# Attention by head in one-bank tiles from one ring of seven, pair loads in 4096-byte pieces, new orders of all lists

## The chip, the cores and the metric

The kernel runs on 1 core of one Trainium2 chip. The metric is device time in microseconds (us) of one execution. Before the change three runs took 1517.64, 1525.69 and 1526.01 us, median 1525.69.

The engines are named as the profile names them: PE (matmul; its weight loads are PEld), DVE (vector), ACT (scalar, activations), POOL (GpSimd) and SP, which here only issues DMA transfers. SBUF is the working memory of 128 partitions; PSUM is the matmul accumulator, eight banks of 2048 bytes in each partition, so that a bank holds 512 floats.

## The reference

The input is `x` of 8 x 512 x 256 (batches, tokens, channels), all in float32. Four residual blocks follow each other, each on a layernorm of `x`:

```python
x = x + block_a(_layernorm(x))     # mamba mixer, then a feed-forward of 4 x 256
x = x + recurrent(_layernorm(x))   # gates over the batch index as time
x = x + attention(_layernorm(x))   # 16 heads of 16 channels, 512 tokens
x = x + recurrent(_layernorm(x))
```

The costly piece of the mamba mixer is a scan over tokens for every channel and each of 16 states:

```python
delta = softplus(dbc[..., :64] @ dt_proj_w + dt_proj_b)
h = exp(delta * A) * h + delta * xc * B       # for each of 16 states
y = einsum('ben,bn->be', h, C)
```

Attention makes, per head, `xw = x_h @ w_att_val`, scores `xw . x_h / sqrt(16)`, a softmax over 512 tokens and the product with `vx = x @ wv_w.T`.

## The kernel before

**Stage one (mamba of all batches, and the first recurrence).** 256 channels x 16 states make 4096 rows of one batch's scan; 128 partitions take 8 channels x 16 states, so a batch has 32 units. ACT makes `dl` (delta) and POOL (DVE for batch 0) makes `dx` (delta * xc), each 128 x 2 x 512. They are stored to DRAM by `store` in `mamba_in` (L338) and read back by `load_unit` (L384), which repeats 8 channels over 16 groups of partitions. A unit takes one load of `dl` and one of `dx`, each 128 pieces of 2048 bytes, 256 KB. Two units in a row share a tile (`dl_rep`, `dx_rep`: three tiles each). Then, per unit: ACT makes the decay `da = exp(A * dl)` into PSUM (`decay`, L391, three banks); POOL makes `bx = dx * B` for a pair of units (`increments`, L398, three tiles); DVE scans (`scan_unit`, L405) and multiplies by C (`times_c`, L411); PE sums the states of four units into `y` (`sum_states`, L421).

**Stage two (attention, with the second recurrence between it).** A step is one batch, one group of four heads and one block of 128 tokens. The scores are made twice: as queries against keys for the row maximum (`s` in the lists: PE L1104 into `ps_s`, `s_`: a DVE reduction into `mp`, L1386), and as keys against queries for the exponential (`e`: PE L1104 into `ps_e`, `e_`: ACT, L1403). A head has 16 channels, padded to 32 rows of PE, so a product uses a quarter of PE's rows. `scores` makes two heads at once into a tile of two banks; three such tiles (tag `two`) are six of the eight banks. All else (transposes, gates, projections) uses the seventh (tag `one`), and the values' sum `po` (`v`: PE L1124) the eighth. Maxima go back into the queries' padding (`m`: PE L1112, `m_`: DVE L1395), so the second product comes out with its maximum subtracted. `k0` to `k3` collect the outputs.

**Orders.** The order of every engine but POOL's own scheduling of waits is written out by hand: `FRONT` (batch 0 begins), `SLOTS` (seven times, one for each boundary), `LAST` and `REST` in stage one, `PROLOGUE`, `GAPS_01` (twice), `GAPS` (six times) and `END` in stage two. A word such as `dl`, `sc` or `e` makes the next piece of that kind; `i.` marks the input half of the next batch, `o.` the output half of the batch before, `e.` the layernorm of the batch after next, `q.` and `r.` the recurrence, `x.` transfers of `x`. Each engine, SP included, runs its own instructions strictly in that order; a wait holds all that stands behind it on the same engine. A tile of a pool is handed out in turn, and its next user waits until its last reader is done.

Of the kernel before, what the change touches and what calls it, by code (L numbers as in the profile page):

```python
# [15 lines left out]
P = 128  # L16
B = 8
# [7 lines left out]
QR = 4  # L25
HC = 8
# [151 lines left out]
def mamba_in(cx, a, t, b):  # L178
# [151 lines left out]
    def store(what, k):  # L330
        if not k:
            d = cx.dram.tile([KC, P, L], F32, tag=what, name=f"{what}_dram_{n}")
            setattr(t, what + "_d", d)
        to, x = (
            y[:, chunk(k), :]
            for y in (getattr(t, what + "_d").rearrange("k p l -> p k l"), getattr(t, what))
        )
        nc.sync.dma_start(to, x)  # L338
# [13 lines left out]
    for k in (None, 0, 1):  # L352
        on = "" if k is None else f".{k}"
        pieces["dx" + on] = lambda k=k: times_input(k)
        for what in ("dl", "dx"):
            pieces[f"store_{what}{on}"] = lambda what=what, k=k: store(what, k)
        if on:
            pieces["silu_x" + on] = lambda k=k: silu_xk(k)
# [9 lines left out]
def unit_channels(u):  # L368


    return u // 16, u % 4, u // 4 % 4


def load_unit(cx, t, b, u, what):

    k, j, r = unit_channels(u)
    pair = getattr(t, what + "_rep")
    if u % 2 == 0:
        pair[u // 2] = cx.rep.tile(
            [P, 2, L], F32, tag=what, bufs=3, name=f"{what}_rep_a{b}_{u}"  # L380
        )
    c0 = j * HP + r * CG
    src = getattr(t, what + "_d")[k, c0 : c0 + CG, :]
    cx.nc.sync.dma_start(  # L384
        pair[u // 2][:, u % 2, :], src.unsqueeze(0).to_broadcast([NS, CG, L])
    )
# [27 lines left out]
def sum_states(cx, a, t, b, quad):  # L414
# [5 lines left out]
    for j in range(4):  # L420
        cx.nc.tensor.matmul(  # L421
            t.y[k][head(j), :],
            a.sum[:, r, :],
            t.hc[4 * quad + j],
            start=False,
            stop=(r == QR - 1),
        )
# [195 lines left out]
def recurrent_step(cx, d, b, tok, tok_tag, ch, ch_tag, t=None, half=None):  # L623
# [9 lines left out]
    def bank(name, tag, bufs=None):  # L633

        if half is None:
            tag, bufs = cx.fill, None
        return cx.psum.tile([P, L], F32, tag=tag, name=name, bufs=bufs)
# [14 lines left out]
    def turn(k):  # L652
# [4 lines left out]
        ps = bank(f"ps_xT_{n}_{k}", ("one", "po")[k])  # L657
# [12 lines left out]
    def inputs(g, m):  # L670
        ps = bank(f"ps_{GATES[g][0]}{m}_{n}", "two", 3)
        ps_of[g, m] = gate_inputs(cx, ps, g, m, t.xT, tk, whole=(b == 0))
# [20 lines left out]
    def act_tile(g, m):  # L693
# [3 lines left out]
        return cx.att.tile([P, 2, L], F32, tag="e", bufs=4, name=f"{what}{m}_{n}")[:, 0, tk]  # L697
# [124 lines left out]
dx q.i0_ a.take_c y q.g0 sc o.gate1 cm i.rms x.load sc sc q.g0_ dl dl dl dx dl dl dl dx dx dx dx dx  # L822
dl dl dx dx dl dx dl dx dx dl da i.scale o.proj0 dx dx dl dx dl q.update0 dl dl o.proj1 i.turn0 q.f1
o.add_proj o.stats i.turn1 q.i1 da i.turn0_ q.f1_ sc i.turn1_ o.norm q.i1_ da cm cm cm q.hold1 y
o.turn0 bx bx e.stats bx bx bx o.residual c.bias bx bx bx o.turn1 o.turn0_ da sc sc o.turn1_ da
i.proj1 o.up0 o.up2 o.up1 da i.proj1_ o.up0_ da o.up2_ o.up1_ da da i.proj0 o.up3 o.up3_ i.proj0_ da
da e.center da sc cm sc cm i.conv1 cm sc da sc cm cm o.down1 y sc i.proj3 o.down0 x.half sc i.proj2
cm o.add1 i.conv0 sc cm sc cm i.silu_x i.silu_z y da i.xproj da i.xproj_ o.up4 dx dl dl dl dl dx dl
dx dx dx dx dl sc dl dx cm sc cm cm cm sc y i.dt1 sc o.add0 i.dt0 o.up5 o.up6 o.up7 da o.up4_ da
e.affine i.dt1_ i.dt0_ bx bx bx da i.dx da o.up5_ da o.up6_ da da o.up7_ da da e.outer da c.gate0 sc  # L830
cm sc cm cm cm sc sc cm y dx o.down3 o.down2 dl i.store_dl i.store_dx dx dl dl dx dl dx q.output0
i.rows dl q.g1 da e.square q.output0_ sc cm sc dx dx sc cm cm sc o.add3 cm cm o.add2 bx bx r.stats
bx e.residual sc sc q.g1_ r.norm cm cm q.update1 q.output1 y da r.turn0 y r.turn1 r.turn0_ da
r.turn1_ da r.f0 sc sc r.f0_ cm x.first sc r.i0 dl dl dx dl dx dl cm sc cm cm r.hold0 dx x.spill bx
da da q.output1_ bx dl dx da
# [4 lines left out]
da dl dx dx q.i0_ da da dl dx dx sc y o.gate1 o.proj0 o.proj1 q.g0 dx dl dl dl dx x.spill dl dx dl  # L840
q.f1 dl dx dl dx dl x.load dx dx q.i1 dl dx dx sc sc o.add_proj bx o.stats a.take_c sc q.g0_ o.norm
sc q.f1_ da cm q.update0 sc cm q.hold1 cm cm dx dl dl dx dl dl dl dx dx dx dl dx dx dl dx dl dl dl
dl dx dx dx dl o.turn1 dl dx dl dl dx o.turn0 y o.turn1_ o.turn0_ bx bx bx o.up0 da da bx o.residual
bx bx bx bx o.up3 o.up1 bx o.up4 o.up2 q.i1_ da o.up0_ da da da q.output1_ o.up3_ o.up1_ da da da
o.up2_ q.output0_ da da o.up4_ da r.output0_ cm sc cm sc sc cm sc cm cm cm sc y sc cm cm y o.down0
o.down1 o.up6 o.up5 o.up7 o.up6_ da da o.up5_ da o.up7_ da da sc sc cm cm sc sc sc o.add0 o.add1 sc
sc cm cm cm y q.output1 o.down2 r.output0 cm sc x.first sc cm cm o.add2 sc sc c.gate0 o.down3 o.add3
r.stats bx cm cm sc y q.g1 cm cm r.output1 r.norm r.turn0 da q.g1_ r.turn0_ q.update1 sc q.output0 y
bx bx bx r.turn1 r.turn1_ da da da r.f0 r.i0 da da da r.i0_ da r.f0_ r.g0 r.f1 r.i1 r.g0_ sc x.half
sc cm sc sc cm r.f1_ r.i1_ sc cm cm r.hold0 cm sc cm r.update0 sc y cm r.hold1 cm  # L850
# [3 lines left out]
o.bias y o.gate1 o.proj0 o.proj1 q.g1 o.add_proj.a o.stats.a o.add_proj.b o.norm.a o.turn0.a  # L854
o.turn1.a o.residual.b o.stats.b o.turn0_.a o.residual.a o.turn1_.a o.up2 o.up0 o.up1 q.g1_
q.output1_ o.up0_ o.up2_ o.up3 o.up1_ o.norm.b o.turn0.b o.up3_ o.turn0_.b o.down0 o.turn1.b o.down1
o.turn1_.b q.update1 o.up7 o.up4 o.add0 o.add1 o.up6 r.stats.a o.up5 o.up4_ o.up6_ o.up5_ r.norm.a
o.up7_ o.down2 o.down3 o.add2 o.add3 r.stats.b
# [3 lines left out]
i.stats i.outer i.center.a i.affine.a i.center.b i.affine.b i.square.a i.square.b i.residual i.rms  # L862
i.scale.a i.scale.b i.turn0 i.turn1 i.turn0_ i.turn1_ i.proj0 i.proj1 i.proj0_ i.proj1_ i.conv0
i.conv1 e.stats i.silu_x.0 i.silu_x.1 i.proj3 i.xproj i.xproj_ i.dt0 i.dt1 i.proj2 i.dt0_ i.dt1_
e.center i.dx.0 i.dx.1 i.rows e.affine i.store_dl.0 i.store_dx.0 i.store_dx.1 dl dx dx e.outer dl dl
da dx i.store_dl.1 e.square bx da da dx dl dx dx dl e.residual bx i.silu_z dx dl dx
# [3 lines left out]
def mamba_and_recurrence(cx, a, w, d):  # L870
# [31 lines left out]
    for b in (5, 6, 7):  # L902
# [3 lines left out]
        "dl": (UNITS, lambda b, n: load_unit(cx, T[b], b, n, "dl")),  # L906
        "dx": (UNITS, lambda b, n: load_unit(cx, T[b], b, n, "dx")),
# [91 lines left out]
def attention_in(cx, c, b, other=None):  # L999
# [6 lines left out]

    def bank(i):
        return other if other and i else cx.fill
# [28 lines left out]
    def turn(k, half):  # L1037
        on, tk, cs = part_of(half)
        ps = cx.psum.tile([P, L], F32, tag=bank(k), bufs=1, name=f"ps_xT_{n}_{k}{on}")
# [600 lines left out]
```

## Time and profile before

The profiled execution took 1520.85 us, of which 1519.1 us is the span from the first instruction to the last; the mean granted TensorE clock was 0.979.

| engine | busy us | share of the span | instructions |
|---|---|---|---|
| PE | 1437.2 | 95% | 6812 |
| PEld | 702.1 | 46% | 6812 |
| DVE | 1086.7 | 72% | 1628 |
| ACT | 836.0 | 55% | 1283 |
| POOL | 501.0 | 33% | 300 |

The costliest groups, as instruction, shape, count, total and mean of one:

| line, engine | what | count | busy us | mean ns |
|---|---|---|---|---|
| L1386 DVE | row maximum, 128x1024 | 256 | 305.5 | 1222 |
| L405 DVE | scan, 128x512 | 256 | 304.6 | 1214 |
| L398 POOL | `bx`, 128x1024 | 128 | 301.5 | 2368 |
| L1403 ACT | exponential of scores, 128x1024 | 256 | 255.2 | 1022 |
| L391 ACT | decay, 128x512 | 256 | 173.7 | 688 |
| L411 DVE | times C, 128x512 | 256 | 164.6 | 674 |
| L1104 PE | scores for `e` | 1024 | 226.3 | 630 |
| L1104 PE | scores for `s` | 1024 | 223.1 | 649 |
| L1124 PE | values | 1024 | 135.5 | 607 |
| L1395 DVE | maximum into queries, 128x512 | 32 | 21.9 | 685 |
| L1142 ACT | copy of `po`, 128x512 | 32 | 18.7 | 584 |

The DMA engines moved 196.77 MB in 112141 packets; the queue that SP issues on was busy for 46.7% of the span. A float32 product is two matmul instructions in the trace, so 512 products of a kind count as 1024. Busy time is the union of a group's instructions: four products that run side by side count once.

### The profile page before, as it was taken

To read this page: it belongs to the slowest core of one execution; us is meant where nothing else is said; L and a number is where in the kernel's file an instruction comes from. 1 tells how busy PE (TensorE), PEld (TensorE's weight loads), DVE (VectorE), ACT (ScalarE), POOL (GpSimd) and SP (SyncE) were. 2 spreads that over 40 slices of the span, in tenths; PEclk is the share of its full clock that TensorE was granted. 3 is DMA by queue.
4 is the path that set the end of the run, shared out by engine and by line. 5 is a ranking of instruction groups with operands and counts; after the bars stand their busy time and mean duration, and the time that the engine had idled before them with its cause. 6 is when DMAs were issued, how large, how long until landed. Compare 5 with 4: busy or idle time off the path is not lost.

```text
span 1519.1 us, 19714 instructions
## 1 busy us (share of the span) xinstructions
PE 1437.2 (95%) x6812; PEld 702.1 (46%) x6812; DVE 1086.7 (72%) x1628; ACT 836.0 (55%) x1283; POOL 501.0 (33%) x300
## 2 busy tenths in 40 slices
PE   4479999999999999999899999999999999999998
PEld 1125455655555555667334443334333333333347
DVE  4799999999999899833766767565656646555326
ACT  5666778676867665522255464645455444554522
POOL 2777777776768566512300000000000000000000
PEclk9699999999999999999799999999999999999999
DMA  7999999899999999703101100100110001110214
GB/s 233 265 260 247 266 241 281 235 265 258 258 260 254 238 253 266 203 1 114 56 19 45 41 17 23 37 19 15 37 23 26 22 15 34 23 37 8 79 68 139
DMA packets 112141, 196.77 MB, mean 130 GB/s; under 512 B 17201, under 2 KB 27761, under 8 KB 112041
## 3 DMA queue, kind: packets, MB, share of 16 engines
q1 hardware_dynamic: 109752, 188.52, 46.7%
q10 hardware_dynamic: 1824, 5.15, 1.0%
q0 software_dynamic: 464, 1.84, 0.3%
q8 instruction: 54, 0.88, 0.2%
q14 instruction: 47, 0.38, 0.1%
HBM read 163.24 MB, written 23.56 MB: 123 GB/s over the span
## 4 chain that ended last, share of the span: by engine, by line
PE 82%; DVE 10%; ACT 3%; issue 2%; DMA 2%; POOL 1%; SPq 0%; ACTq 0%; DVEq 0%; POOLq 0%
PE ps_e_c L1104 10%; PE ps_s_c L1104 10%; PE ps_o_c L1124 8%; PE ps_f_o L522 6%; PE ps_f_o L498 6%; DVE hc_a L405 3%; PE y_a L421 3%; PE ps_in_a L245 3%; PE ps_w_c L1204 2%; PE ps_f_d L599 2%; PE ps_i_d L599 2%; PE ps_g_d L599 2%; DVE hc_a L411 2%; PE ps_v_c L1070 2%; PE ps_f_d L612 2%
## 5 line engine op out<-in xcount | busy, mean ns | idle before, releaser
L1386 DVE TENSOR_REDUCE mp<-ps_s_c 128x2 f32<-128x1024 f32 x256 | 305.5, 1222 | 174.0 <-PE ps_s_c L1104 125.5
L1403 ACT ACTIVATE e_c<-ps_e_c 128x1024 f32<-128x1024 f32 x256 | 255.2, 1022 | 221.3 <-PE ps_e_c L1104 146.4
L398 POOL TENSOR_TENSOR bx_a<-dx_rep_a,B_a 128x1024 f32<-128x1024 f32 x128 | 301.5, 2368 | 107.0 <-DMA dx_rep_a<-dx_dram_a 55.7
L405 DVE TENSOR_TENSOR_SCAN hc_a<-da_a,bx_a 128x512 f32<-128x512 f32 x256 | 304.6, 1214 | 20.2 <-POOL bx_a L398 9.6
L391 ACT ACTIVATE da_a<-dl_rep_a,neg_a 128x512 f32<-128x512 f32 x256 | 173.7, 688 | 113.9 <-DMA dl_rep_a<-dl_dram_a 64.3
L1104 PE MATMUL ps_e_c<-q_c,keys 32*128 32x512 f32 x1024 | 226.3, 630 | 0.7 <-DVE q_c L1395 0.7
L1104 PE MATMUL ps_s_c<-keys,q_c 32*128 32x512 f32 x1024 | 223.1, 649 | 3.0 <-DVE mp L1386 1.7
L411 DVE TENSOR_TENSOR hc_a<-hc_a,Cp_a 128x512 f32<-128x512 f32 x256 | 164.6, 674 | 0.0
L85 POOL TENSOR_TENSOR rs_d<-ve_d,neg_half 128x4 f32<-128x4 f32 x8 | 8.1, 1015 | 404.1 <-DVE ve_d L84 212.9
L1124 PE MATMUL ps_o_c<-e_c,va 128*32 128x512 f32 x1024 | 135.5, 607 | 0.0
L498 PE MATMUL ps_f_o<-h_o,w 128*128 128x256 f32 x512 | 116.6, 381 | 1.3 <-ACT f_o L511 0.8
L1104 PEld LDWEIGHTS ps_e_c<-q_c,keys 32*128 32x128 f32 x1024 | 68.5, 183 | 101.4 <-issue 52.9
L522 PE MATMUL ps_f_o<-w,f_o 128*128 128x256 f32 x512 | 115.1, 381 | 0.0
L498 PEld LDWEIGHTS ps_f_o<-h_o,w 128*128 128x128 f32 x512 | 96.2, 190 | 28.6 <-ACT da_a L391 6.8
L522 PEld LDWEIGHTS ps_f_o<-w,f_o 128*128 128x128 f32 x512 | 96.4, 190 | 22.1 <-ACT da_a L391 5.0
L421 PE MATMUL y_a<-hc_a,sum 128*32 128x512 f32 x512 | 90.1, 625 | 15.5 <-DVE hc_a L411 15.5
L1104 PEld LDWEIGHTS ps_s_c<-keys,q_c 32*128 32x128 f32 x1024 | 65.8, 187 | 72.5 <-issue 29.9
L85 POOL TENSOR_TENSOR rs_c<-ve_c,neg_half 128x4 f32<-128x4 f32 x7 | 7.1, 1010 | 217.6 <-DVE ve_c L84 217.6
L511 ACT ACTIVATE f_o<-ps_f_o,vecs 128x256 f32<-128x256 f32 x128 | 53.0, 467 | 23.4 <-PE ps_f_o L498 23.4
L245 PE MATMUL ps_in_a<-hT_a,w_in 128*128 128x512 f32 x128 | 65.0, 638 | 0.4 <-ACT dl_a L307 0.4
L1124 PEld LDWEIGHTS ps_o_c<-e_c,va 128*32 128x32 f32 x1024 | 21.6, 108 | 89.6 <-issue 87.1
L115 PE MATMUL ps_hT_a<-ident,h_a 128*128 128x128 f32 x64 | 13.4, 332 | 37.0 <-ACT h_a L225 35.9
(317 smaller groups left out, 1974.8 us busy)
## 6 DMA issues: line engine op xcount, KB each, us to landing
dl_rep_a<-dl_dram_a SPq DMA_DIRECT2D x256, 256.0 KB
dx_rep_a<-dx_dram_a SPq DMA_DIRECT2D x256, 256.0 KB
x<-in_x_dram SPq DMA_DIRECT2D x8, 512.0 KB
keys<-xT_c SPq DMA_DIRECT2D x128, 32.0 KB
o_c<-oT_c SPq DMA_DIRECT2D x128, 32.0 KB
xT_dram_d<-xT_d SPq DMA_DIRECT2D x8, 512.0 KB
xT_back<-xT_dram_d SPq DMA_DIRECT2D x8, 512.0 KB
sum_c<-inverse_c SPq DMA_DIRECT2D x15, 256.0 KB
```

The costliest lines, as they stand in the source:

```text
L245: nc.tensor.matmul(ps, a.in_proj[:, k, ts(m, P)], t.hT[:, k, :], start=(k == 0), stop=(k == KC - 1))
L391: cx.nc.scalar.activation(t.da[u], t.dl_rep[u // 2][:, u % 2, :], AF.Exp, scale=a.A[:, u : u + 1])
L398: cx.nc.gpsimd.tensor_mul(t.bx[pair], t.dx_rep[pair], t.B.unsqueeze(1).to_broadcast([P, 2, L]))
L405: cx.nc.vector.tensor_tensor_scan(t.hc[u], t.da[u], t.bx[u // 2][:, u % 2, :], 0.0, ALU.mult, ALU.add)
L411: cx.nc.vector.tensor_mul(t.hc[u], t.hc[u], t.Cp)
L421: cx.nc.tensor.matmul(t.y[k][head(j), :], a.sum[:, r, :], t.hc[4 * quad + j], start=False, stop=(r == QR - 1),)
L498: nc.tensor.matmul(ps[:, m, :], a.w1[:, k, ts(m0 + m, P)], t.h2[:, k, ts(half, L // 2)], start=(k == 0), stop=(k == KC - 1),)
L522: nc.tensor.matmul(ps, t.f[c // 2][:, m, ts(c % 2, P)], a.w2[:, m, :], start=(m == 0), stop=(m == FC - 1),)
L1104: cx.nc.tensor.matmul(ps[:, j, :], lhs[rows, :], rhs[rows, :], start=True, stop=True)
L1124: cx.nc.tensor.matmul(po[head(j), :], c.va[b % 2][:, t, g * HG + j, :], es[j // 2][:, j % 2, :], start=(t == 0), stop=(t == TC - 1),)
L1386: nc.vector.tensor_reduce(c.mp[:, t, h : h + 2, DH], ps.pop(("s", b, g, t, i)), AX.X, ALU.max, negate=True)
L1403: nc.scalar.activation(e, ps.pop(("e", b, g, t, i)), AF.Exp)
```

## The change

1. **Pair loads.** The DRAM copies of `dl` and `dx` are laid out so that channels c and c + 64 of a chunk of 128 stand beside each other. One load then brings both units of a pair, in 128 pieces of 4096 bytes (512 KB), and there are 256 loads in place of 512. The units of a quad come in the order of `QUAD`; `A_log` and the rows of `y` follow it. The stores write 2 x 64 x 512 in DRAM from 128 partitions, always one chunk at a time: 32 stores of 256 KB in place of 4 of 256 KB and 14 of 512 KB.
2. **Attention by head.** `scores` makes one head into one bank. Each reduction, exponential and query copy is 128x512, and there are twice as many. All PSUM tiles of the stage but `po` come from one ring of seven banks (tag `bank`). The `e` tiles are eight of 128x512 in place of four of 128x1024.
3. **Orders.** All seven lists are new. In `SLOTS` the stores, written as `i.store_dl i.store_dx`, become four single ones.

No arithmetic is added or left out; POOL and PE run as many instructions as before (3630 products on PE), DVE 256 more, ACT 271 more, SP 242 fewer.

```diff
     def store(what, k):
         if not k:
-            d = cx.dram.tile([KC, P, L], F32, tag=what, name=f"{what}_dram_{n}")
+            d = cx.dram.tile([KC, P // 2, 2, L], F32, tag=what, name=f"{what}_dram_{n}")
             setattr(t, what + "_d", d)
-        to, x = (
-            y[:, chunk(k), :]
-            for y in (getattr(t, what + "_d").rearrange("k p l -> p k l"), getattr(t, what))
-        )
-        nc.sync.dma_start(to, x)
+        to = getattr(t, what + "_d")[k].rearrange("c h l -> h c l")
+        nc.sync.dma_start(to, getattr(t, what)[:, k, :])
...
-def load_unit(cx, t, b, u, what):
-
-    k, j, r = unit_channels(u)
-    pair = getattr(t, what + "_rep")
-    if u % 2 == 0:
-        pair[u // 2] = cx.rep.tile(
-            [P, 2, L], F32, tag=what, bufs=3, name=f"{what}_rep_a{b}_{u}"
-        )
+def load_pair(cx, t, b, pair, what):
+
+    k, r, j = pair // 8, pair // 2 % QR, pair % 2
+    rep = cx.rep.tile([P, 2, L], F32, tag=what, bufs=3, name=f"{what}_rep_a{b}_{2 * pair}")
+    getattr(t, what + "_rep")[pair] = rep
     c0 = j * HP + r * CG
-    src = getattr(t, what + "_d")[k, c0 : c0 + CG, :]
-    cx.nc.sync.dma_start(
-        pair[u // 2][:, u % 2, :], src.unsqueeze(0).to_broadcast([NS, CG, L])
-    )
+    src = getattr(t, what + "_d")[k, c0 : c0 + CG]
+    cx.nc.sync.dma_start(rep, src.unsqueeze(0).to_broadcast([NS, CG, 2, L]))
...
             t.y[k][head(QUAD[j]), :],
...
 SLOTS = """
...
-cm sc cm cm cm sc sc cm y dx o.down3 o.down2 dl i.store_dl i.store_dx dx dl dl dx dl dx q.output0
-i.rows dl q.g1 da e.square q.output0_ sc cm sc dx dx sc cm cm sc o.add3 cm cm o.add2 bx bx r.stats
...
+q.output0 dl dx sc q.g1 cm sc sc cm sc cm sc sc i.dx da sc cm o.add2 da q.output0_ bx c.bias o.add3
+q.output1 q.g1_ i.store_dx.0 i.store_dl.0 r.stats bx cm cm cm cm dl i.store_dl.1 i.rows dx
+i.store_dx.1 dx dl dx y y q.update1 r.norm r.turn0 r.turn1 r.turn0_ r.turn1_ r.f0 da da r.f0_ sc sc
+sc cm cm sc cm dx dl x.spill da q.output1_ da bx bx x.first r.i0 r.hold0 cm
...
-def scores(cx, name, lhs, rhs, i):
-
-    ps = cx.psum.tile([P, 2, L], F32, tag="two", bufs=3, name=f"{name}_{i}")
-    for j in range(2):
-        rows = head(2 * i + j)
-        cx.nc.tensor.matmul(ps[:, j, :], lhs[rows, :], rhs[rows, :], start=True, stop=True)
+def scores(cx, name, lhs, rhs, j):
+
+    ps = cx.psum.tile([P, L], F32, tag=cx.fill, name=f"{name}_{j}")
+    cx.nc.tensor.matmul(ps, lhs[head(j), :], rhs[head(j), :], start=True, stop=True)
     return ps
...
     def row_max_(b, g, t, i):
-        h = g * HG + 2 * i
-        nc.vector.tensor_reduce(
-            c.mp[:, t, h : h + 2, DH], ps.pop(("s", b, g, t, i)), AX.X, ALU.max, negate=True
-        )
+        to = c.mp[:, t, g * HG + i, DH : DH + 1]
+        nc.vector.tensor_reduce(to, ps.pop(("s", b, g, t, i)), AX.X, ALU.max, negate=True)
...
     def attend_(b, g, t, i):
-        e = cx.att.tile([P, 2, L], F32, tag="e", bufs=4, name=f"e_c{b}_{g}_{t}_{i}")
+        e = cx.att.tile([P, L], F32, tag="e", bufs=8, name=f"e_c{b}_{g}_{t}_{i}")
         nc.scalar.activation(e, ps.pop(("e", b, g, t, i)), AF.Exp)
...
-            cx.psum = pool(st2, "c_psum", 1, space=PSUM)
-            cx.fill = "one"
+            cx.psum = pool(st2, "c_psum", 7, space=PSUM)
+            cx.fill = "bank"
```

## The prediction

> **What bounds the kernel now.** I first cut the span where its character changes: the busy time of every engine in six stretches.
>
> ```profile
> core 0: us, PE busy (x) PEld busy (x) DVE busy (x) ACT busy (x) POOL busy (x), PEclk, DMA share, GB/s
> 0.00:52.00 52.00, 16.10 (x32) 6.34 (x32) 20.94 (x55) 31.47 (x58) 19.49 (x24) 0.87 0.77 243
> 100.00:576.00 476.00, 461.35 (x1859) 268.89 (x1860) 455.66 (x707) 338.16 (x602) 344.84 (x181) 0.99 0.99 256
> 760.00:1435.00 675.00, 672.23 (x3850) 256.24 (x3848) 402.41 (x536) 344.52 (x414) 28.65 (x26) 1.00 0.10 27
> ```
>
> From 100 to 576 us (mamba) DVE is busy for 455.66 of 476 us, and DMA's share is 0.99 at 256 GB/s. Two resources look full, so I asked what DVE waited for there:
>
> ```profile
> DVE hc_a L405 <- ACT da_a L391: 7.0, 11, 1.6
> DVE u_a L457 <- PE ps_op_o L445: 3.0, 4, 0.7
> DVE ps_g_b L712 <- ACT ps_g_b L618: 2.1, 4, 0.6
> ```
>
> The largest entry is 7.0 us, and none names a transfer. DVE is the bound; DMA is full but prefetched far enough ahead. The loads can give DVE at most the 7.0 us.
>
> From 760 to 1435 us (attention) PE is busy for 672 of 675 us. A busy PE need not be at its peak, so I looked at its order:
>
> ```profile
> 1005.87 0.70 PE L1104 MATMUL ps_e_c<-q_c,keys 32*128 32x512 f32 x2
> 1005.88 0.70 PE L1104 MATMUL ps_s_c<-keys,q_c 32*128 32x512 f32 x2
> 1006.40 0.59 PE L1104 MATMUL ps_e_c<-q_c,keys 32*128 32x512 f32 x2
> 1006.42 1.44 PE L1104 MATMUL ps_s_c<-keys,q_c 32*128 32x512 f32 x6
> 1007.79 1.06 PE L1124 MATMUL ps_o_c<-e_c,va 128*32 128x512 f32 x8
> 1008.78 1.14 PE L1104 MATMUL ps_s_c<-keys,q_c 32*128 32x512 f32 x8
> 1009.75 1.02 PE L1104 MATMUL ps_e_c<-q_c,keys 32*128 32x512 f32 x4
> 1010.70 0.64 PE L1124 MATMUL ps_o_c<-e_c,va 128*32 128x512 f32 x4
> ```
>
> Each score product is two matmul instructions on one group of 32 rows. Four products on four groups run side by side: from 1008.78 the x8 take 0.97 us before the next x4 start, and those two products alone take 0.95. So a run of scores costs rounds, not products. Six products in two rounds last 1.92 us (1008.78 to 1010.70); the eight instructions of values before them last 0.99. With 0.86 us a round, 0.2 remains for each change between the 32-row form and another. Attention is this sum, with hardly any wait.
>
> **The attention part.** I counted PE's order in both programs from the first score to the last values. Before: 210 runs of scores holding 296 rounds, 139 runs of full-array products, 115 of values. After: 182 runs, 289 rounds, 68 full-array runs, 123 of values. Rounds: 7 x 0.86 = 6.0 us. Runs of scores: 28 x 0.2 = 5.6. Full-array runs: 71 x 0.18, if they change as dearly as the scores do, = 12.8. Values: 8 x 0.13 = 1.0 back (0.99 less one round). Together -23.4 us.
>
> The price is in the evacuations, which double in number. The 128x1024 reduction takes 1222 ns; a 128x512 read of PSUM on DVE takes about 685 (the addition at L1395), so 256 x (2 x 685 - 1222) = +38 us on DVE. On ACT the exponential goes from 1022 to about 584 (the 128x512 copy at L1142): 256 x 146 = +37 us. Against 675 us DVE goes to 440 and ACT to 382, both beside PE, whose order hides them while banks come free in time. A ring of seven hands out banks strictly in turn, so the late evacuation of any one holds PE. After counts 71 runs of seven scores, which use the whole ring. A wait of 0.07 us for each is +5; I take -18 us, with ends -23 and 0.
>
> **The loads.** 512 loads of 128 pieces of 2048 bytes become 256 loads of 128 pieces of 4096. In the mamba stretch the SP queue moved 117.98 MB in 96.2% of 16 x 476 us, that is 127 ns for 2048 bytes. For 4096 I use a lone transfer at 1461 us (window 1.8 us), and for the number of engines a lone one at 844 us (window 2.3 us from 843.90, its first line the busy tenths in forty slices). The lines of the SP queue in the three DMA views:
>
> ```profile
> q1 hardware_dynamic: 64856, 117.98, 96.2%
> ```
> ```profile
> DMA packets 144, 0.52 MB, mean 291 GB/s; under 512 B 16, under 2 KB 16, under 8 KB 144
> ...
> q1 hardware_dynamic: 144, 0.52, 71.2%
> ```
> ```profile
> DMA  0000099020212244464375446446423320320000
> ...
> DMA packets 136, 0.26 MB, mean 114 GB/s; under 512 B 8, under 2 KB 8, under 8 KB 136
> ...
> q1 hardware_dynamic: 136, 0.26, 35.8%
> ```
>
> The first lone one (128 pieces of 4096): 0.712 x 16 x 1.8 / 128 = 160 ns each. So the loads fall from 512 x 128 x 0.127 / 16 = 520 us of the engines to 256 x 128 x 0.160 / 16 = 328. DVE did not wait for them, so that buys part of the 7.0 us: -3 (0 to -7).
>
> The Trainium skill, DMA: Bandwidth & Descriptors, Specifications, puts the least size for line rate at 512 bytes; by that rule pieces of 4096 would gain nothing over 2048. Here a byte in 4096 cost 39 ps against 62 in the loaded stretch, so the measurement decides; by the page's rule the term of -3 would be 0.
>
> **The stores** are where I expect the loss. To let two channels stand side by side in DRAM, each store now writes 2 x 64 x 512 from 128 partitions: its outermost count is 2, where it was 128. The second lone transfer is `sum_c<-inverse_c` (L1188), whose source is 8 x 16 x 512. It has 8 small completion packets; the first, 128 rows on both sides, has 16. So 8 outermost ran on 8 engines, and I read 2 as two engines. A store of 128 pieces of 2048 bytes is then 64 pieces on each of two, not 8 on each of sixteen. A piece costs between 80 ns (half of 160) and 103 (0.358 x 16 x 2.3 us / 128, in the lone transfer at 844 us); I take 90, nearer the lone rows, since fourteen engines are idle then: 5.8 us a store.
>
> The Trainium skill, same page, section "Why a DMA increments its semaphore by 16 and not by 1", says that a transfer takes the largest number up to 16 that divides the outermost counts of both sides. For 2 and 128 this is 2; it speaks against this change.
>
> Four such stores stand at each batch boundary, and everything behind them on those two rings waits. After's order on SP: store dx.0, store dl.0, load dl of pair 0, store dl.1, B, C, load dx of pair 0, store dx.1, load dx of pair 1. From the first issue (0 us; 1.4 us to the first packet: L1188 was issued at 842.80, and its first busy slice begins at 844.19): two stores end at 13.0. SP sits in the wait of the dl load meanwhile, with all that follows queued behind it. That load: 1.4 to start, 8 x 0.16 to move, 15.8. Store dl.1: 21.6. B and C, 16 x 0.09: 23.0. dx of pair 0: 24.3. POOL's product (2.37): 26.7, and only then can the new batch's first scan start. Then dx.1 to 30.1, dx of pair 1 to 31.4, its product to 33.8.
>
> What covers this is DVE's own work. At the first issue POOL has just made dx, two products of 2.37 after the scan of unit 21; in DVE's order there remain 7 scans at 1.13 (start to start), 10 products with C at 0.59, two residual additions (0.7), statistics (2.3), three gate products (1.8) and the copy of C (0.6): 19.2 us. Before, the same stretch was covered: store at 479.67, first new scan at 499.05, no wait. Now DVE stands from 19.2 to 26.7 = 7.5 us, then from 29.6 (two scans and a gate) to 33.8 = 4.2. 11.7 us at 7 boundaries = +82. With 80 ns a piece the same sum gives 8.8 x 7 = +62; with 103, 15.1 x 7 = +106.
>
> In the front, two stores (13.0 us) precede the first dx load: first scan 18.2 us after the first store against 11.8 before (35.09 to 46.88), and the third store delays pair 1 by about 3 more: +9 (0 to +16).
>
> The other reordering (rms, conv, LAST, REST) moves the same instructions; from 576 to 760 us DVE's main wait is 25.9 us for `ps_f_o`, which stays PE's. I cost it at 0 and include +-5.
>
> **Sum:** 82 + 9 - 18 - 3 = +70 on the profiled 1520.85 us (span 1519.1 and 1.75 around it; 0.3% under the median of 1525.69): 1591 us.
>
> **Rivals.** (1) The stores are not slow: they spread over four engines or more. With four (2.9 us a store) the first scan could start at 18 us, inside the 19.2, so this is the point from which it decides. Left are -18, -3 and 0 to -5: 1497 us, faster. For it: no transfer here shows an outermost 2. Against: 8 gave 8.
> (2) The ring holds PE: with the stores hidden, 0.3 us at each of the 71 runs of seven = +21, which cancels the -23: 1516 us, no change. Against: DVE and ACT have a third of the stretch free.
> (3) DVE's cover is longer than 19.2 because it runs late at the boundary: the stall shrinks to the second one, 4.2 x 7 = 29, with +9 - 21: 1538.
>
> **Numbers.** Stores slow and exposed: 75%, own range 1555 (62 + 4 - 25 - 7) to 1643 (106 + 16). Rival 1: 17%, rival 2: 6%, rival 3: 2%. The range for 8 in 10 must reach into rival 1: 1497 to 1643. About 1% (15 us) is what a measurement of this kernel tells from no change: faster 0.17, same 0.07, slower 0.76.
>
> **What would show it.** After's stores with 2 small completion packets, 5 to 7 us long on an eighth of the engines; DVE's waits at `hc_a` for POOL's `bx_a` or ACT's `da_a` near 80 us from 50 to 600 us, twice a boundary; attention 15 to 23 us shorter. I am wrong if the stores land in under 3 us, if DVE stays at 96% between the boundaries and at them, or if PE shows waits at the scores for DVE or ACT of over 20 us.

## The result, and the profile after

The changed kernel takes 1699.48 us (median of 4, 1697.93 to 1702.38) against 1525.47 for the kernel before beside it: a ratio of 1.1156, 95% interval 1.1117 to 1.1196. The forecast was 1591 with a range up to 1643: the direction held, the size did not. The profiled execution has a span of 1696.1 us.

| us | before | after | difference | predicted |
|---|---|---|---|---|
| up to the first scan | 46.9 | 53.5 | +6.6 | +9 |
| first scan to the first score | 682.7 | 882.5 | +199.8 | +79 (stores 82, loads -3) |
| first score to the last values | 702.9 | 673.7 | -29.2 | -18 |
| the rest | 86.6 | 86.4 | -0.2 | 0 |

The same cut of the span as before the change; mamba now runs to about 780 us, and attention from 960. Columns: busy time and instructions of each engine, granted clock, DMA share, GB/s.

```profile
core 0: us, PE busy (x) PEld busy (x) DVE busy (x) ACT busy (x) POOL busy (x), PEclk, DMA share, GB/s
0.00:52.00 52.00, 14.62 (x32) 5.86 (x32) 18.05 (x52) 28.58 (x55) 15.27 (x22) 0.87 0.64 204
100.00:780.00 680.00, 527.98 (x1910) 297.19 (x1910) 476.67 (x728) 346.50 (x616) 355.63 (x185) 0.87 0.77 188
960.00:1600.00 640.00, 638.87 (x3796) 264.92 (x3794) 425.34 (x787) 355.93 (x663) 32.17 (x28) 1.00 0.10 27
```

DVE, which bounded mamba, is now idle for 203 of 680 us there (680 - 476.67), where it was idle for 20 of 476. DMA's share has fallen too, from 0.99 to 0.77: the transfers are neither the full resource they were nor ahead of the work. In attention PE is as busy as it was, in a shorter stretch. What DVE waits for from 100 to 780 us (us in total, times, longest):

```profile
DVE hc_a L393 <- ACT da_a L379: 61.4, 21, 12.4
DVE hc_a L393 <- POOL bx_a L386: 45.1, 13, 8.9
DVE Cp_a L320 <- DMA C_a<-bc_a: 29.5, 5, 13.8
DVE act_f_b L689 <- ACT ps_f_b L606: 24.9, 9, 5.6
```

The scan (`hc_a`) waits for ACT's decay and POOL's product, and these wait for loads. Their lines before, then after (count, busy us, mean ns; then the engine's idle time before them, and what ended most of it):

```profile
L391 ACT ACTIVATE da_a<-dl_rep_a,neg_a 128x512 f32<-128x512 f32 x256 | 173.7, 688 | 113.9 <-DMA dl_rep_a<-dl_dram_a 64.3
L398 POOL TENSOR_TENSOR bx_a<-dx_rep_a,B_a 128x1024 f32<-128x1024 f32 x128 | 301.5, 2368 | 107.0 <-DMA dx_rep_a<-dx_dram_a 55.7
```
```profile
L379 ACT ACTIVATE da_a<-dl_rep_a,neg_a 128x512 f32<-128x512 f32 x256 | 169.8, 686 | 318.2 <-DMA dl_rep_a<-dl_dram_a 273.1
L386 POOL TENSOR_TENSOR bx_a<-dx_rep_a,B_a 128x1024 f32<-128x1024 f32 x128 | 300.5, 2355 | 314.5 <-DMA dx_rep_a<-dx_dram_a 272.3
```

The copy of C waits for its load, which stands behind the stores on SP. PE's granted clock fell as well, from 0.99 to 0.87, but DVE waits for PE itself for only 13.5 of the 203 us. One boundary on SP's queue (start, duration of the issue, what is issued), and the DMA engines' work while SP is silent:

```profile
324.13 0.54 SPq L336 DMA_DIRECT2D dx_dram_a<-dx_a  x1
324.73 0.53 SPq L336 DMA_DIRECT2D dl_dram_a<-dl_a  x1
338.75 0.58 SPq L374 DMA_DIRECT2D dl_rep_a<-dl_dram_a  x1
339.38 0.51 SPq L336 DMA_DIRECT2D dl_dram_a<-dl_a  x1
339.93 0.57 SPq L314 DMA_DIRECT2D B_a<-bc_a  x1
```
```profile
DMA  1111111111111111111111111111111111111111
...
DMA packets 202, 0.41 MB, mean 51 GB/s; under 512 B 2, under 2 KB 2, under 8 KB 202
...
q1 hardware_dynamic: 202, 0.41, 13.1%
```

Between 324.73 and 338.75 SP issues nothing: the load of `dl` waits for the store that it reads. The second view is 329 to 337 us within that gap: 51 GB/s at a share of 13.1%, that is 2.1 of 16 engines. SP's waits of that kind from 60 to 800 us (us in total, times, longest):

```profile
SPq L374 <- DMA dl_dram_a<-dl_a: 95.9, 8, 14.8
```

The stores do run on two engines, as the Trainium skill has it (DMA: Bandwidth & Descriptors, "Why a DMA increments its semaphore by 16 and not by 1") and as the prediction took it: 200 pieces in 8 us on two engines are 80 ns each, 5.1 us for a store of 128 (predicted 5.8).

### The profile page after: what moved, and what is told of

The parts are those of the page before. It is cut to its first block, busy times and chain, and to the rows that moved or that the text cites. A ratio compares the mean times of both kernels' runs of the same rounds, so it can differ in the third digit from the quotient of the medians.

```text
span 1696.1 us, 19885 instructions
## 1 busy us (share of the span) xinstructions
PE 1458.0 (86%) x6812; PEld 739.3 (44%) x6812; DVE 1107.3 (65%) x1884; ACT 852.8 (50%) x1554; POOL 498.8 (29%) x300
## 4 chain that ended last, share of the span: by engine, by line
PE 55%; DMA 25%; POOL 6%; DVE 5%; ACT 5%; SPq 2%; issue 2%; ACTq 0%; POOLq 0%; DVEq 0%
DMA dx_rep_a<-dx_dram_a 10%; PE ps_e_c L1085 9%; DMA dl_rep_a<-dl_dram_a 9%; PE ps_s_c L1085 8%; PE ps_o_c L1105 7%; DMA dl_dram_a<-dl_a 6%; POOL bx_a L386 4%; PE ps_f_o L486 3%; PE ps_v_c L1053 2%; PE ps_w_c L1185 2%; PE ps_f_o L510 2%; DVE hc_a L393 2%; PE ps_f_d L587 2%; PE ps_g_d L587 2%; PE ps_i_d L587 2%
## 5 line engine op out<-in xcount | busy, mean ns | idle before, releaser
L1374 DVE TENSOR_REDUCE mp<-ps_s_c 128x1 f32<-128x512 f32 x512 | 324.9, 683 | 162.8 <-PE ps_s_c L1085 140.5
L1389 ACT ACTIVATE e_c<-ps_e_c 128x512 f32<-128x512 f32 x512 | 279.7, 600 | 168.2 <-PE ps_s_c L1085 105.9
L1085 PE MATMUL ps_e_c<-q_c,keys 32*128 32x512 f32 x1024 | 289.0, 626 | 0.0
L1085 PE MATMUL ps_s_c<-keys,q_c 32*128 32x512 f32 x1024 | 279.7, 626 | 0.6 <-DMA keys<-xT_c 0.6
L409 PE MATMUL y_a<-hc_a,sum 128*32 128x512 f32 x512 | 104.7, 673 | 46.5 <-DVE hc_a L399 46.5
L1085 PEld LDWEIGHTS ps_e_c<-q_c,keys 32*128 32x128 f32 x1024 | 98.5, 183 | 84.4 <-issue 34.0
L1085 PEld LDWEIGHTS ps_s_c<-keys,q_c 32*128 32x128 f32 x1024 | 95.1, 183 | 78.8 <-issue 22.8
L433 PE MATMUL ps_op_o<-w_op,zs_a 128*128 128x256 f32 x128 | 49.7, 548 | 91.6 <-ACT act_i_b L606 51.5
L433 PEld LDWEIGHTS ps_op_o<-w_op,zs_a 128*128 128x128 f32 x128 | 33.9, 278 | 109.4 <-ACT act_i_b L606 55.2
L409 PEld LDWEIGHTS y_a<-hc_a,sum 128*32 128x32 f32 x512 | 16.5, 113 | 117.2 <-DVE hc_a L399 77.5
```

The source lines that it names most:

```text
L409: cx.nc.tensor.matmul(t.y[k][head(QUAD[j]), :], a.sum[:, r, :], t.hc[4 * quad + j], start=False, stop=(r == QR - 1),)
L1085: cx.nc.tensor.matmul(ps, lhs[head(j), :], rhs[head(j), :], start=True, stop=True)
L1374: nc.vector.tensor_reduce(to, ps.pop(("s", b, g, t, i)), AX.X, ALU.max, negate=True)
L1389: nc.scalar.activation(e, ps.pop(("e", b, g, t, i)), AF.Exp)
```

## The experiments

Eighteen runs; those of one group shared a chip and the runs of the kernel before on it (medians of before 1524.1 to 1526.8 us), so runs of different groups are best compared by their ratios. "Old" orders are SLOTS, LAST, REST and FRONT of before; the attention is that of after in all runs but e2. "The ring", here and in the recorded expectations, is the 16 DMA engines taken together (the ring of seven is PSUM's). "Piece" is the mean duration of a DMA piece of the loads' size in the trace from 60 to 560 us.

| run | orders | stores | load pieces, rows read | us | ratio to before [95%] | piece, ns |
|---|---|---|---|---|---|---|
| after | new | two engines | 4096, 8 rows x16 | 1699.5 | 1.1156 [1.1117, 1.1196] | 273 |
| e1 | new | halves | 4096, 8 x16 | 1586.5 | 1.0395 [1.0368, 1.0423] | 273 |
| e3 | new | dl halves, dx two engines | 4096, 8 x16 | 1639.9 | 1.0750 [1.0726, 1.0775] | 275 |
| e5 | new | halves | 2048, 8 x16 | 1540.4 | 1.0098 [1.0068, 1.0128] | 122 |
| e4 | old | before's | 2048, 8 x16 | 1495.3 | 0.9806 [0.9783, 0.9829] | 129 |
| e8 | old | halves | 4096, 8 x16 | 1538.8 | 1.0093 [1.0070, 1.0117] | 274 |
| e2 | old, old attention | two engines | 2048, 8 x16 | 1654.6 | 1.0850 [1.0829, 1.0872] | 127 |
| e7 | new | halves | 4096, 64 x2 | 1498.3 | 0.9835 [0.9794, 0.9876] | 192 |
| e21 | new | halves | 2048, 64 x2 | 1499.2 | 0.9838 [0.9807, 0.9869] | 100 |
| e14 | old | before's | 2048, 64 x2 | 1487.8 | 0.9752 [0.9736, 0.9768] | 98 |
| e15 | new | halves | 4096, 16 x8 | 1579.8 | 1.0347 [1.0328, 1.0365] | 268 |
| e18 | new | halves | 4096, 16 x8, apart | 1580.9 | 1.0374 [1.0339, 1.0409] | 260 |
| e17 | new | halves | 4096, 8 x16, apart | 1588.8 | 1.0425 [1.0392, 1.0458] | 271 |
| e19 | old | before's | 2048, 8 x16, apart | 1499.2 | 0.9837 [0.9809, 0.9865] | 117 |
| e9 | new, `i.dx` early | two engines | 4096, 8 x16 | 1700.9 | 1.1153 [1.1125, 1.1181] | 274 |
| e12 | new, stores ahead | two engines | 4096, 8 x16 | 1686.7 | 1.1052 [1.1035, 1.1068] | 270 |
| e11 | new, stores ahead | halves | 2048, 8 x16 | 1539.9 | 1.0085 [1.0070, 1.0100] | 124 |
| e16 | new, loads in turn | halves | 2048, 8 x16 | 1537.0 | 1.0067 [1.0042, 1.0092] | 121 |
| e20 | e16, old boundary | halves | 2048, 8 x16 | 1526.3 | 1.0008 [0.9991, 1.0026] | 126 |

**The stores: undone (e1), half undone (e3), and alone on the kernel before (e2).**

```diff
-        nc.sync.dma_start(to, getattr(t, what)[:, k, :])
+        for h in range(2):
+            nc.sync.dma_start(to[h], getattr(t, what)[ts(h, P // 2), k, :])
```

> All of the change, but each store of 128 x 512 goes out as two transfers of 64 rows, so that the outermost count of both sides is 64 and not 2. Theory A (a store whose outermost count is 2 runs on two engines, and holds all loads behind it; this makes the whole +200 us from the first scan to the first score): sixteen engines per store, that stretch returns to 675 to 690 us (before 682.7, after 882.5), 32 scans take 75 to 77 us (before 76, after 103), and with the attention 29 us shorter and the front 5 us longer the time is 1500 us (1488 to 1512). Rival B (loads of 4096-byte pieces, which take 275 ns under load, or the new orders of the lists hold the scans): the stretch stays over 730 us and the time over 1545.

1586.5. The stores are worth 113 us (1699.5 - 1586.5), the front's part among them, but 62 us over before remain although the attention gives 29 back: rival B is in part right too.

In e3 the same edit is made for `what == "dl"` alone.

> As the run with every store in two transfers of 64 rows, but for the dl stores alone: the two dx stores of a boundary keep their outermost count of 2. It is the half dose. Theory A1 (what is lost is the transfer capacity of the ring: 5.3 us for each slow store at 2 of 16 engines, wherever it lies, since the transfers had no slack): half of the loss returns, the time is 1600 us (1580 to 1620). Theory A2 (what is lost is latency: the wait of the first scan past the work that covers it, so the first 5 us of a pair cost nothing and the last ones all): more than half returns, 1540 us (1515 to 1570). Rival B (stores cost little): 1680 or more.

1639.9: 53 of the 113 are left with half of the slow stores. The loss goes with the dose, as A1 has it (half of 113 would leave 1643); the first slow store of a boundary is not free. (A1's own 1600 started from the wrong end, 1500 instead of 1586.)

In e2 the kernel before gets stores with an outermost count of 2:

```diff
-            d = cx.dram.tile([KC, P, L], F32, tag=what, name=f"{what}_dram_{n}")
+            d = cx.dram.tile([KC, 2, P // 2 + 1, L], F32, tag=what, name=f"{what}_dram_{n}")
...
-        nc.sync.dma_start(to, x)
+        to = getattr(t, what + "_d")[:, :, : P // 2, :].rearrange("k h c l -> h c k l")
+        for one in (0, 1) if k is None else (k,):
+            nc.sync.dma_start(to[:, :, one, :], getattr(t, what)[:, one, :])
```

> Before, its orders, loads and attention untouched, but each of its two stores of a batch written as two transfers of 128 pieces of 2048 bytes whose outermost count is 2 (the DRAM tensor is padded so that the halves stay apart). One part of the change alone. Latency: four stores of 5.3 us take 21 us from the first packet, then a load, then POOL's product of 2.4: first new scan 28 us after the first store against 19.4 of cover: 9 x 7 = 63 and 10 in the front, 1598 (1580 to 1620). Capacity: 18.5 us of the ring lost at each boundary whose transfers were full: 130 and 10, 1665 (1645 to 1690). If outermost counts do not matter at all: 1525.

1654.6, +130, within the capacity case and outside the latency case. One period of e2, then one of before, each from a boundary's first store to the next boundary's; the second window ends at the new batch's first scan:

```profile
388.80:412.00 23.20, 14.83 (x71) 9.57 (x69) 13.21 (x26) 9.04 (x21) 7.01 (x5) 0.93 0.46 138
412.00:424.70 12.70, 8.83 (x20) 3.71 (x24) 6.98 (x9) 5.19 (x9) 8.62 (x4) 0.72 0.90 260
424.70:444.30 19.60, 19.60 (x77) 10.34 (x70) 17.63 (x39) 11.63 (x22) 10.35 (x10) 1.00 0.76 233
444.30:483.50 39.20, 39.20 (x168) 25.59 (x167) 37.70 (x46) 31.08 (x52) 30.82 (x14) 1.00 1.02 247
```
```profile
402.80:408.00 5.20, 5.20 (x21) 3.77 (x20) 5.20 (x12) 4.45 (x10) 5.20 (x3) 1.00 1.00 332
408.00:421.50 13.50, 12.72 (x48) 4.68 (x50) 13.43 (x23) 8.45 (x18) 9.71 (x7) 1.00 1.01 263
421.50:441.00 19.50, 19.50 (x77) 10.34 (x70) 17.63 (x40) 12.10 (x22) 11.06 (x10) 1.00 0.90 261
441.00:479.70 38.70, 38.70 (x166) 25.17 (x165) 37.25 (x46) 31.05 (x52) 30.82 (x14) 1.00 1.01 245
```

From the new batch's first scan to the next store both take 58 to 59 us. From store to first scan e2 takes 35.9 and before 18.7. In e2's first 23.2 us DVE is busy for 13.21: the scans that were to cover the stores starved (`hc_a` waits 15.0 us for `da_a` up to the first new scan), since in before's order the old batch's last three loads stand behind the stores on SP. So hardly anything of the stores' time is covered: the ring loses 4 x 5.1 x 14/16 = 17.9 us, and the period grows by 17.8 (94.7 - 76.9). The mean over six periods is 16.9 in e2, and 14.6 between e1 and after (103.9 - 89.2), where the new orders put these loads ahead of the stores. What e2 does not separate is the ring's lost time from the place of those three loads.

Two runs moved after's own slow stores ahead, to see whether cover helps: in e9 `i.dx` goes behind `i.dt1_` and the first two stores behind the old batch's last two pair loads; in e12 ahead of these loads.

The lists of e12 around the moved entries:

```diff
-i.dt0_ i.dt1_ y o.up5
+i.dt0_ i.dt1_ i.dx y o.up5
...
-q.output0 dl dx sc
+q.output0 i.store_dx.0 i.store_dl.0 dl dx sc
...
-sc sc i.dx da sc
+sc sc da sc
...
-q.g1_ i.store_dx.0 i.store_dl.0 r.stats
+q.g1_ r.stats
```

> After itself, with its slow stores, but in SLOTS i.dx stands right behind i.dt1_ and the first two stores right behind the last two pair loads of the old batch: nine more scans then lie between the first store and the new batch's first scan. If the stores cost by their latency past the cover, some 11 us of cover a boundary return at 7 boundaries: 1699 - 77 = 1622 (1600 to 1645). If they cost by capacity (a store on two engines takes the ring from loads that are never caught up), the place doesn't matter: 1685 or more.

> After itself with its slow stores, with the same move: i.dx behind i.dt1_, and the first two stores ahead of the old batch's last pair loads on SP. Moving only behind those loads left the first store where it was (4 to 6 scans before the new batch), so that run told nothing; this one does move it. Latency past the cover: two more scans with their products, some 7 us at 7 boundaries: 1650 (1630 to 1670). Capacity (the ring loses the time wherever the slow stores stand): 1685 or more.

1700.9 and 1686.7: e9 gives nothing back, e12 13 to 16 of the 113 us. By the numbers this is the capacity case, in e12 at its edge, but neither is a clean test: the first store still found 4 to 6 scans left, since `i.dx` on POOL stays behind the same products `bx` (in e9 SP waited 3.4 us for it, up to 430.2). Whether a slow store far enough ahead would be hidden was not tried.

**The pieces, and the orders.** e4 is before with the attention of after; e5 is e1 with each pair load as two loads of 2048-byte pieces; e8 is e1 with SLOTS, LAST, REST and FRONT of before, two unit loads made one pair load.

```diff
-    cx.nc.sync.dma_start(rep, src.unsqueeze(0).to_broadcast([NS, CG, 2, L]))
+    for h in range(2):
+        cx.nc.sync.dma_start(
+            rep[:, h, :], src[:, h, :].unsqueeze(0).to_broadcast([NS, CG, L])
+        )
```

> The attention of after (one-bank tiles from the ring of seven, its GAPS) with the stores, loads and lists SLOTS, LAST, REST and FRONT of before. If the attention's gain is its own, first score to last values takes 674 us as in after (before 702.9) and the time is 1497 us (1490 to 1503). Rival (part of the 29 us came from the longer stage ahead of it, which left evacuations or loads done early): the time is 1506 or more. With theory A it lies within 10 us of the run that has all of the change with stores in halves; if the new lists or the pair loads are worth something themselves, that run is the faster by over 10 us, and if they cost, the slower.

1495.3; its attention takes 673.9 us. The gain of 29 is the attention's own, and this is the fastest run here that computes everything. No run divides it between the one-bank tiles and the new order of PE.

> As the run with every store in halves, and each pair load as two loads of 128 pieces of 2048 bytes (before's size), in the same place of the order. If a piece of 4096 takes twice as long as one of 2048 under load (275 against 127 ns, as after's trace has it), the transfers' share and the time stay as in the run with halves alone, within 6 us. If a byte in the larger piece is cheaper, as my prediction had it (160 ns for 4096), this run has a DMA share from 100 to 500 us that is higher by over 0.1, and it is slower by 3 us or more.

1540.4, that is 46 us faster with the smaller pieces. Neither theory said so: the large piece takes 273 ns where two small ones take 245. Over 256 loads of 128 pieces these 28 ns are 57 us of the 16 engines.

> Completes the square of orders and piece sizes: the pair loads of 4096-byte pieces, stores in halves and attention of after, but SLOTS, LAST, REST and FRONT of before (each two unit loads of a list become one pair load, in the first one's place). So far: old orders with 2048 bytes 1495, new orders with 2048 bytes 1540, new orders with 4096 bytes 1586. Capacity (a 4096-byte piece takes 272 ns among others against twice 129, and before's transfers were full at a share of 0.99: 272/258 = 1.055 on 609 us of scans): +33 on 1495 = 1528 (1518 to 1540), DMA share still about 1.0. Additive (sizes and orders independent, +46): 1541. Cover (old orders have enough work laid ahead to hide later landings): 1495 to 1508.

1538.8. The square closes: from 1495.3, the new orders cost 45, the large pieces cost 44, both together 91 (1586.5). The two costs add up; 1538.8 also lies at the upper end of the capacity case, whose own figure (16 ns a piece, 33 us) is 11 short of the 44. One rival stays open: with small pieces a pair's `dl` comes as two loads, and the first decay needs only the first. ACT's idle time for `dl` in the whole trace is 166.5 us in e1 and 116.8 in e5; how much of the 44 to 46 us is this earlier landing was not measured. DMA in e8, e1 and e7 from 200 to 500 us:

```profile
DMA packets 22556, 72.24 MB, mean 241 GB/s; under 512 B 2592, under 2 KB 4128, under 8 KB 22536
...
q1 hardware_dynamic: 21768, 69.64, 96.8%
```
```profile
DMA packets 21624, 67.09 MB, mean 224 GB/s; under 512 B 2544, under 2 KB 4080, under 8 KB 21606
...
q1 hardware_dynamic: 20886, 64.59, 87.5%
```
```profile
DMA packets 23585, 74.64 MB, mean 249 GB/s; under 512 B 2736, under 2 KB 4272, under 8 KB 23564
...
q1 hardware_dynamic: 22796, 72.03, 71.2%
```

e8, with the old orders, is full: SP's queue alone has 96.8% and moves 69.64 MB. In e1, with the new ones, a tenth of the engines' time is left over although DVE waits for loads. The third, e7, moves more than either in 71.2%.

**What makes a piece slow.** e7 reads 64 rows twice each, where the kernel reads 8 rows sixteen times.

```diff
-    src = getattr(t, what + "_d")[k, c0 : c0 + CG]
-    cx.nc.sync.dma_start(rep, src.unsqueeze(0).to_broadcast([NS, CG, 2, L]))
+    src = getattr(t, what + "_d")[k].rearrange("c h l -> c (h l)")
+    src = src.unsqueeze(1).to_broadcast([P // 2, 2, 2 * L])
+    cx.nc.sync.dma_start(rep.rearrange("p h l -> p (h l)"), src)
```

> As the run with every store in halves, with pair loads of the same 128 pieces of 4096 bytes, but each load reads 64 rows of the chunk twice each where the kernel reads 8 rows sixteen times each (so dl and dx that are scanned are of other channels: the output is not the reference's). If many engines reading the same few rows is what makes a 4096-byte piece take 272 ns among others and 159 alone, the mean falls below 220 ns and the time to 1550 or less. If it is the sum of the traffic, the mean stays at 255 to 285 ns and the time at 1576 to 1596.

192 ns and 1498.3: the re-reading costs 88 us of e1. e14 is the same on e4's unit loads.

> As the run with the attention alone (old orders, unit loads of 128 pieces of 2048 bytes), but each load reads 64 rows twice each instead of 8 rows sixteen times (the output is not the reference's). If sharing rows slows pieces of 2048 bytes too, their mean falls from 129 ns to 90 to 110, the DMA share from 1.0 to 0.7 to 0.87, and the time by the little that DVE waited, to 1478 to 1490. If only pieces of 4096 bytes suffer, mean and share stay and the time is 1495.

98 ns and 1487.8: small pieces suffer too, but before has them ahead of DVE, so only 7 to 8 us show. Four runs asked what about the re-reading is slow: e15 gives each engine a row of its own, eight times; e18 takes these 16 rows 16 KB apart; e17 puts the kernel's own 8 rows 32 KB apart, and e19 does so with e4's.

```diff
+    src = getattr(t, what + "_d")[k].rearrange("c h l -> c (h l)")[ts(pair % 4, NS)]
+    src = src.unsqueeze(1).to_broadcast([NS, CG, 2 * L])
...
-            d = cx.dram.tile([KC, P // 2, 2, L], F32, tag=what, name=f"{what}_dram_{n}")
+            d = cx.dram.tile([KC, P // 2, 8, 2, L], F32, tag=what, name=f"{what}_dram_{n}")
```

> As the run with every store in halves, with pair loads of the same 128 pieces of 4096 bytes, but each load reads 16 rows eight times each, with the row as the outermost count: an engine reads one row eight times, and no two engines read the same row (channels are again others, the output is not the reference's). The kernel reads 8 rows sixteen times, with every engine going through the same 8 rows. If what is slow is that engines read the same row at the same time, the mean piece falls to 180 to 220 ns, as with 64 rows twice (191.5), and the time to 1490 to 1515. If reading a row over and over is slow by itself, the mean stays at 255 to 285 ns and the time at 1575 to 1595.

> As the run in which each engine reads its own row eight times (268 ns a piece, 1580 us), but the 16 rows of a load are every fourth of the 64, 16 KB apart: the same 256 KB of DRAM that the run with 64 rows twice spans (191.5 ns, 1498 us). If the span decides: 180 to 220 ns and 1490 to 1515. If the number of times that a row is read decides: 255 to 285 ns and 1570 to 1590.

> As the run with every store in halves, but in DRAM the rows of 4096 bytes stand 32 KB apart, so that the 8 rows that a load reads sixteen times span 256 KB and not 32. If the narrow span of DRAM is what slows the pieces, their mean falls from 272 ns to 180 to 225 as with 64 rows read twice, and the time from 1586 to 1495 to 1515. If reading a row many times is what slows them, mean and time stay: 260 to 285 ns, 1575 to 1595.

> The run with the attention alone (1495), with the rows of 2048 bytes 32 KB apart in DRAM; the result is the reference's. If the span decides, pieces fall from 129 ns to 90 to 105 as with 64 rows twice, and the time to 1483 to 1491, the fastest that computes everything. If repetition decides: 120 to 135 ns and 1490 to 1500.

e15: 268 ns, 1579.8. e18: 260 ns, 1580.9. e17: 271 ns, 1588.8. e19: 117 ns, 1499.2. For pieces of 4096 bytes neither engines meeting at a row nor the span of DRAM is it. For those of 2048 the span gives back 12 of the 31 ns between 129 and 98, and nothing of the time. What goes with the speed is how often a row is read in a load (2 against 8 and 16). In these runs that is the same as how many different rows a load has (64 against 16 and 8), so the two are not told apart; where in the memory it is decided stays open.

**The orders.** e11 makes e12's move on e5; e16 lets e5's 25 loads of a batch take turns, dl then dx; e20 adds before's sequence of stores and first loads to e16.

What e20 changes on e16, beside `i.dx`:

```diff
-q.output0 dx dl sc
+q.output0 i.store_dl.0 i.store_dl.1 i.store_dx.0 i.store_dx.1 dx dl sc
...
-q.g1_ i.store_dx.0 i.store_dl.0 r.stats bx cm cm cm cm dl i.store_dl.1 i.rows dx i.store_dx.1 dx dl dx
+q.g1_ r.stats bx cm cm cm cm dx i.rows dl dx dl dx
```

> As the run with stores in halves and pieces of 2048 bytes (1540), but in SLOTS i.dx stands right behind i.dt1_, and store dx.0 and store dl.0 ahead of the loads of the old batch's last pair, so that on SP they no longer wait for that pair's buffers. In the runs with the old orders 7 scans are left at the first store, with the new ones 4 to 6. If that late store is what the new orders cost (45 us), 6 or 7 scans are left and the time is 1500 to 1518. If it is something else in the orders: 1530 or more.

> As the run with stores in halves and pieces of 2048 bytes (1540), but the 25 loads of a batch ahead of its successor's store take turns, dl then dx, where SLOTS of after has four dx in a row and then four dl. If SP standing at a dx load whose buffer is not free, with the dl load that the next scan needs behind it, is what the new orders cost: 1500 to 1518. If not: 1530 or more.

> As the run with the loads in turn (1537), and around a boundary SP has before's sequence as well: all four stores together ahead of the old batch's last pair loads, then dx of the new pair 0, B, C, dl of pair 0 (after has dl of pair 0, a store, B, C, dx of pair 0, a store). If SP's sequence is what the new orders cost: 1495 to 1515. If it is the order of the work on the other engines: 1528 or more.

1539.9, 1537.0 and 1526.3: all three miss the gain asked for. In e11 the first store still found 4 to 6 scans left, so it did not test its own question; in e20 it found 7 or 8. The sequence on SP gives back 14 of the 45 us, 11 of them by the boundary's part in e20 (e16 alone is within the noise of e5); the rest lies elsewhere. e21 asks from the other side, with e5's loads reading 64 rows twice:

> The new orders with stores in halves and pieces of 2048 bytes (1540), but each load reads 64 rows twice each (the output is not the reference's). The old orders with such loads took 1487.8. If the new orders cost only through the waits for loads: 1485 to 1497. If they cost by the compute that they put in the way: 1515 or more.

1499.2 against 1487.8 for the old orders with such loads (two groups of runs, before at 1524.1 and 1526.8): 11 to 14 us remain of 45. What DVE waited for in e5, and in e21, from 60 to 560 us:

```profile
DVE hc_a L397 <- POOL bx_a L390: 18.7, 9, 4.3
DVE ps_g_b L702 <- ACT act_i_b L610: 15.2, 5, 3.6
DVE hc_a L397 <- ACT da_a L383: 8.6, 10, 3.9
```
```profile
DVE ps_g_b L702 <- ACT act_i_b L610: 7.1, 4, 3.3
DVE u_a L449 <- PE ps_op_o L437: 6.1, 4, 1.8
DVE hc_a L397 <- ACT da_a L383: 3.9, 6, 1.2
DVE hc_a L397 <- POOL bx_a L390: 3.4, 2, 3.1
```

With cheap loads the scans' waits fall from 27.3 to 7.3 us and the gate's (`ps_g_b`) by half. In e5 POOL at such a boundary shows where they come from, its first product of the new batch:

```profile
358.94 2.36 POOL L390 TENSOR_TENSOR bx_a<-dx_rep_a,B_a 128x1024 f32<-128x1024 f32 x1
369.40 2.36 POOL L390 TENSOR_TENSOR bx_a<-dx_rep_a,B_a 128x1024 f32<-128x1024 f32 x1 [8.09 <-DMA dx_rep_a<-dx_dram_a]
```

8.09 us idle for a load. So 31 to 34 of the orders' 45 us go when loads are cheap, and are read here as waits for loads that come later than under the old orders; which moves of the other engines' lists make them late is not settled.

## Why the prediction was wrong

- **What bounds the kernel.** "The loads can give DVE at most the 7.0 us" was true and beside the point: the loads could not give much, but they could take. DMA's share of 0.99 was read as full but far enough ahead. In e2 17.9 us taken from the ring came out as 17.8 us of the period shown, 16.9 in the mean. DVE's list of waits names only the last link: behind ACT's decay stood 64.3 us of waiting for `dl`, and behind POOL's product 55.7 for `dx`, in before's own profile (the lines above). This reading is the step that failed, and three terms rest on it.
- **The stores, +82 and +9 in the front.** The mechanism held (two engines, 5.1 us), and so, roughly, did the chain: the first scan came 31 to 33 us after the first store, 26.7 predicted. Together they are 113, 22 more than the two terms. A period lost 14.6 us, not 11.7. In the traces, as means of six periods, DVE is idle for 15.1 of the 31.5 us to the new batch's first scan (7.5 predicted), where e1 with its fast stores idles for 3.7 of 20.0. Two figures of the chain and the cover were off. The 1.4 us from issue to first packet came from a lone transfer; at these seven boundaries the first store's packets began 2.5 to 5.1 us after its issue, behind loads still queued on the ring. And DVE had 4 to 6 scans left, not 7, 16.4 us of work and not 19.2. On the kernel before, with its 7 scans, slow stores cost 130. The ring's loss of 17.9 us a boundary is the price that the working never formed.
- **The loads, -3.** They cost about 45 (e1 - e5 46, e8 - e4 44). The mis-sized figure is the 160 ns for 4096 bytes, from a lone store (`xT_dram_d<-xT_d`); among other loads, with each row read sixteen times, it is 273. The 127 ns for 2048 came from the loaded stretch and from rows read sixteen times, so two patterns were compared. Traffic beside a piece explains little: three stores of `x` in before's loaded stretch, of 4096-byte pieces, take 165 to 173 ns. The Trainium skill's rule (DMA: Bandwidth & Descriptors, Specifications: line rate from 512 bytes) would have made the term 0, and with rows read twice it is, within some 6 us: 1498.3 with 4096, 1499.2 with 2048. With rows read sixteen times the measurement decides, against the rule and against the term. That larger pieces lose, no view of before showed.
- **The other reordering, 0 and ±5.** It cost 45 (e5 - e4) beside dear loads and 11 to 14 beside cheap ones. "The same instructions" were moved, but in a stage whose transfers were full the order decides whether the ring stands idle: a tenth of it did in e1 and hardly any in e8.
- **The attention, -18.** -29.2, outside the ends of -23 and 0. The count of rounds and runs alone gave -23.4; the +5 for a ring that holds PE was wrong. PE's waits from 960 to 1600 us, all of them:

```profile
PE ps_w_c L1185 <- DVE o_c L1179: 0.7, 1, 0.7
PE ps_o_c L1105 <- ACT oT_c L1123: 0.3, 1, 0.3
```

  No wait at the scores. Weight loads do wait for evacuations there, up to 0.8 us at a time, under running products. The other 5.8 us of the gain were not divided further.
- **The rivals.** (1) fell with the two engines, (2) with PE's two waits, (3) with a cover that was shorter (16.4 us), not longer.

The sum as measured, in the steps after, e1, e5, e4, before: stores 113, pieces 46, orders 45, attention -29, which is 175 = 1699.5 - 1524.4. Of the 105 that are missing from the predicted 70, 49 are the pieces' (46 + 3), 45 the orders', 22 the stores', and the attention gave 11 more.

## What to carry to other kernels

Where a stage shows its transfers at a share near 1, price every edit of transfers in ring time (engines taken x duration), not by the stall that is left behind some cover, and ask whether the covering work itself waits in that queue. Take both durations of a comparison from the same load and the same pattern of reads. Follow a busy engine's waits one link further back before calling a full resource harmless. The change's attention without its other parts (e4, 1495.3 us) is what to keep.

## What the runs showed of the hardware

- A piece of a load that reads 8 rows sixteen times takes 129 ns for 2048 bytes and 273 for 4096; with 64 rows twice each 98 and 192 (means under load). Eight reads of each of 16 rows by one engine each are hardly better than sixteen (268), and 16 or 32 KB between the rows change little for large pieces (260, 271) and bring small ones to 117.
- Under that load one piece of 4096 bytes takes longer than two of 2048 (273 against 245 in the same orders), and the change of size costs 44 to 46 us here; with rows read twice the two sizes take the same time within some 6 us.
- A store with an outermost count of 2 ran on two engines, 5.1 us for 256 KB at 51 GB/s.
